# Where weights, bands and image buffers begin in memory: a convolution with an involution behind it, on one core

## The chip, the cores and the metric

The kernel runs on one core of a Trainium2 chip. Times are microseconds (us) on the device; the kernel before takes 1350.81 us, the median of three runs. The core has a matrix engine (TensorE, "PE" in the profile, its weight loads "PEld"), VectorE ("DVE"), ScalarE ("ACT"), GpSimd ("POOL") and SyncE ("SP"). 16 DMA engines move data between DRAM and the on-chip memory SBUF, which has 128 partitions.

## The reference

Two layers over 32 images of 256 channels and 32 x 32 pixels, in float32. The first normalizes groups of 8 channels, rounds to half precision, and adds a 3 x 3 convolution. The second makes from its own input, for every pixel and each of 16 groups of channels, the 49 weights of a 7 x 7 window, and sums the window with them (an involution):

```python
x = x + conv3x3(_gn(x))                                   # 256 -> 256 channels, quantized
v = _gn(x)
y = relu(bn(einsum('oc,bchw->bohw', w1, v)))              # 64 channels
w = einsum('oc,bchw->bohw', w2, y) + b2                   # 16 groups x 49 weights a pixel
patches = [pad(v, 3)[:, :, i:i+H, j:j+W] for i in range(7) for j in range(7)]
x = x + einsum('bgkhw,bgckhw->bgchw', w, patches)
```

## The kernel before

The first layer of one image, its second normalization and the transposing of its pixels (`front`) run a few steps ahead of the second layer. One loop over `n` (L559) deals out the work by hand: in every other step a piece of the convolution (L332, 9 matmuls), the sums of one window (L525, 64 matmuls), weights of four rows (L414, 16 matmuls into each of two tiles), and, where due, transposes (L399) or the 64-channel product (L380). An image has `M` = 8 windows, one for each of `K` = 4 strips of 8 rows and two `SIDES` of 16 columns.

A sum over a window is made as a matmul: the contraction runs over pixels that give (partitions), and its moving operand is a band, which holds for every giving pixel the weights with which it enters the pixels around it. The weights must therefore be sheared, and this is done through DRAM:

- `weights` (L406) makes the weights in PSUM with one row of pixels on the partitions; `evict` (L427) adds the bias and places them in `w_sb`, a ring of 32 rows in SBUF with 160 floats (`WB`, 640 bytes) a row.
- `scatter` (L468) sends them to `wd` in DRAM, seven DMAs for each strip, all from SyncE (L479), 896 in all. One DMA takes 32 partitions and 8 rows, so 256 runs of 640 bytes. In `wd` a pixel has `WPIX` = 7 x 160 + 8 = 1128 floats (4512 bytes): seven rows of weights and eight zeros behind them.
- `load_bands` (L481) brings a strip back into one of three bands, with 16 DMAs (L500), two from SyncE and 14 from GpSimd. Each takes 8 rows and both sides, 16 runs of up to 1128 floats. Row `r` begins `2 r` floats ahead of its pixel, which shifts the weights by that many places; what is then read before the pixel is the zeros behind its neighbour. Successive DMAs of GpSimd share eight semaphores: the ninth waits until the first has landed.

A band has, on each side, room for 22 columns of 160 floats; a window uses 19 of them (`WINI`): columns 3 to 21 on side 0 and 0 to 18 on side 1. `sums` (L511) picks them with `j0`. The ring and the bands are filled with zeros once by GpSimd (L144, L196, L198), and three DMAs write the zeros in `wd` that are never overwritten (L191). `x_tiles` holds five images of 8192 bytes a partition; `load_x` fills one with two DMAs (L106), `add_windows` (L541) adds the sums to it, and `store` (L546) writes it out in two halves.

SyncE's queue takes, in order of issue, scatters, two loads of each band, loads of x and stores. The addresses of the program before, in bytes within a partition: bands at 14048, 42272 and 70496, the ring at 117152, the x buffers from 172896 on in steps of 8192. `wd` begins at 81920 in DRAM.

Of the kernel before, what the change touches and what calls it, by code (L numbers as in the profile page):

```python
# [9 lines left out]
F32 = mybir.dt.float32  # L10
# [3 lines left out]
P = 128  # L14
B, C, H, W = 32, 256, 32, 32
# [5 lines left out]
K1, PAD1 = 7, 3  # L21
# [15 lines left out]
XR = 4  # L37
RG = 2
KP = P // RG
TR = RG * XR  # L40
SIDES = 2
JC = W // SIDES
K = H // TR
M = K * SIDES
WIN = XR + K1 - 1
WINC = JC + K1 - 1
WINI = JC + PAD1

V = 2
A = G // V
WB = G * WIN
PAD = V * (TR - XR)
WPIX = K1 * WB + PAD
SW = K1 * G
S = H + 2 * PAD1
T = 4
# [2 lines left out]
PAIRS = G // 2  # L62
ROW = S * WPIX
WR = 4
NBAND = 3
# [13 lines left out]
def tile_quant_conv_then_involution(  # L79
# [10 lines left out]
    nc = tc.nc  # L90
    PSUM = bass.MemoryType.PSUM

    const = ctx.enter_context(tc.tile_pool(name="const", bufs=1))
# [45 lines left out]
        nc.gpsimd.memset(t, 0.0)  # L139

    y_sb = [const.tile([P, N // 2], F32, name=f"y_{i}") for i in range(2)]
    bands = [const.tile([P, SIDES, WINC * WB + PAD], F32, name=f"band_{i}") for i in range(NBAND)]
    for t in bands[CH:]:
        nc.gpsimd.memset(t, 0.0)  # L144
    pixels = [const.tile([P, 2, PAIRS, PAIR], F32, name=f"pixels_{i}") for i in range(NPIX)]
# [4 lines left out]
    w_sb = const.tile([P, 2, RING, A, WIN, V], F32, name="w_sb")  # L150
    wd = dram.tile([H, S, WPIX], F32, name="wd")
    acc = [ps_acc.tile([P, RG, NT], F32, name=f"acc_{d}") for d in range(SIDES)]
# [15 lines left out]
    w2_sb = late_sb[:, : K1 * SW].rearrange("p (k n) -> p k n", n=SW)  # L168
    b2_sb = late_sb[:, K1 * SW :].rearrange("p (e r n) -> p e r n", r=2, n=SW)

    bn_ve = const.tile([P, 1], F32, name="bn_ve")
    nc.vector.tensor_scalar(bn_ve, bn[:, 3:4], BN_EPS, None, ALU.add)
    bn_r = rsqrt(bn_ve, [P, 1], "bn")
# [5 lines left out]


    for col, cols, at, n in (
        (0, S, K1 * WB, PAD),
        (PAD1, PAD1, 0, PAD1 * WB),
        (W, PAD1, (K1 - PAD1) * WB, PAD1 * WB),
    ):
        to = bass.AP(
            tensor=wd.tensor,
            offset=wd.offset + col * WPIX + at,
            ap=[[ROW, H], [WPIX, cols], [1, n]],
        )  # L190
        nc.sync.dma_start(to, bands[NBAND - 1][:H, 0, :n].unsqueeze(1).to_broadcast([H, cols, n]))  # L191
# [276 lines left out]
    def scatter(b, k, part):  # L468

        at = (b * H + k * TR) % RING  # L470
        for dj in range(part, K1, 2):
            t, e = divmod(dj, 2)
            to = bass.AP(
                tensor=wd.tensor,
                offset=wd.offset + k * TR * ROW + dj * WPIX + (K1 - 1 - dj) * WB,
                ap=[[WPIX, TW], [ROW, TR], [1, WB]],
            )
            rows = w_sb[t * TW : (t + 1) * TW, e, at : at + TR]
            nc.sync.dma_start(to, rows.rearrange("p s a r v -> p s (a r v)"))  # L479

    def load_bands(b, k):  # L481

        band = bands[(b * K + k) % NBAND]
        side = WINC * WB + PAD
        for i, j in enumerate(ORDER):
            cut = max(0, PAD1 - j)
            n = (K1 - cut) * WB + PAD
            src = bass.AP(
                tensor=wd.tensor,
                offset=wd.offset + k * TR * ROW + (j + PAD1) * WPIX + cut * WB,  # L490
                ap=[[ROW - V, TR], [(W - 1 - 2 * j) * WPIX - cut * WB, SIDES], [1, n]],
            )
            to = band[j::JC]
            to = bass.AP(
                tensor=to.tensor,
                offset=to.offset + (j + cut) * WB,
                ap=[to.ap[0], [side + (JC - 1 - 2 * j - cut) * WB, SIDES], [1, n]],
            )
            queue = nc.sync if j in BY_SYNC else nc.gpsimd
            queue.dma_start(to, src)  # L500

    def windows(b, m):


        k, d = divmod(m, SIDES)
        for g in range(RG):
            top = k * TR + g * XR - PAD1
            at = acc[d][:, g, : CH * WINI * WIN].rearrange("p (h j r) -> p h j r", h=CH, r=WIN)
            yield g, at, top, max(top, 0), min(top + WIN, H)

    def sums(b, m):  # L511

        k, d = divmod(m, SIDES)
        j0 = 0 if d else PAD1
        band = bands[(b * K + k) % NBAND][:, d]
        px = pixels[(b * K + k) % NPIX][:, d]
        for h in range(CH):
            for v in range(2):
                for g, at, top, f, l in windows(b, m):
                    p = slice(g * KP, (g + 1) * KP)  # L520
                    of = band[p, V * g * XR + j0 * WB : V * g * XR + (j0 + WINI) * WB]
                    of = of.rearrange("p (j a r v) -> p j a r v", a=A, r=WIN, v=V)
                    for t in range(T):
                        a = h * T + t
                        nc.tensor.matmul(  # L525
                            at[t * TW : (t + 1) * TW, h, :, f - top : l - top],
                            px[p, a, v * GC : v * GC + TW],
                            of[:, :, a, f - top : l - top, v],
                            start=(h, v) == (0, 0),
                            stop=(h, v) == (CH - 1, 1),  # L530
                        )

    def add_windows(b, m):
# [4 lines left out]
        for g, at, top, f, l in windows(b, m):  # L538
            x_at = to[:, :, f:l, j0 : j0 + WINI]
            of = at.rearrange("p h j r -> p h r j")[:, :, f - top : l - top]  # L540
# [11 lines left out]
    def due(n, lag):  # L552

        b, i = divmod(n - lag, per)
        return (b, i) if 0 <= b < B else (None, None)

    with tc.manual_schedule():
        fronts = {}
        for n in range(FRONT, B * per + 2):  # L559
            b, i = due(n, FRONT)  # L560
# [12 lines left out]
            b, i = due(n, 0)  # L573
            if b is not None and i % 2 == 0:
                sums(b, i // 2)
            b, i = due(n, 1)
# [6 lines left out]
            b, i = due(n, 2)  # L583
            if b is not None and i == 2 * (M - 1 - SIDES):
                store(b, 0)
            b, i = due(n, -LEAD)
# [3 lines left out]
            for part in range(2):  # L590
                b, i = due(n, -LEAD + 1 + part)
                if b is not None and i % 2 == 0:
                    for k in range(K):
                        if i // 2 == min((k + 1) * TR // WR, H // WR - 1):
                            scatter(b, k, part)
            b, i = due(n, LOAD)
# [3 lines left out]
            b, i = due(n, 3 - 4 * NBAND)  # L600
            if b is not None and i % 4 == 0:
                load_bands(b, i // 4)
# [38 lines left out]
```

## Time and profile before

| what | value |
|---|---|
| three runs | 1348.24, 1350.81, 1355.07 us |
| the profiled execution | 1362.92 us, span 1361.1 us |
| mean granted TensorE clock | 0.98 |
| GpSimd's issues of bands (L500) | 1792, 549 ns each, 980.4 us |
| from such an issue to landing | median 4.5 us (2.5 to 8.6) |
| scatter issues on SyncE (L479) | 896, 160 KB each, median 526 ns |
| HBM | 176.60 MB read, 180.76 MB written |

The profile is of one execution. A share of busy time is an average; which resource sets the time of a stretch is read from what ended the waits there. "Issue" in a list of waits means that nothing in the trace held the engine.

### The profile page before, as it was taken

To read this page: it belongs to the slowest core of one execution; us is meant where nothing else is said; L and a number is where in the kernel's file an instruction comes from. 1 tells how busy PE (TensorE), PEld (TensorE's weight loads), DVE (VectorE), ACT (ScalarE), POOL (GpSimd) and SP (SyncE) were. 2 spreads that over 40 slices of the span, in tenths; PEclk is the share of its full clock that TensorE was granted. 3 is DMA by queue.
4 is the path that set the end of the run, shared out by engine and by line. 5 is a ranking of instruction groups with operands and counts; after the bars stand their busy time and mean duration, and the time that the engine had idled before them with its cause. 6 is when DMAs were issued, how large, how long until landed. Compare 5 with 4: busy or idle time off the path is not lost.

```text
span 1361.1 us, 69383 instructions
## 1 busy us (share of the span) xinstructions
PE 1264.5 (93%) x29440; PEld 808.0 (59%) x29440; DVE 819.7 (60%) x2539; ACT 733.2 (54%) x1731; POOL 1014.4 (75%) x1818
## 2 busy tenths in 40 slices
PE   5899999999999999999999999999999999999765
PEld 2455666665656665665666566666666665666543
DVE  3465666565657665665566566666666665666542
ACT  6765656455655555655456555546555554653300
POOL 9067877777786786787778777777777777888785
PEclk9999999999999999999999999999999999999986
DMA  6099999999999999999999999999999999999995
GB/s 225 20 250 254 280 270 288 281 278 265 280 267 271 289 278 270 282 281 270 284 272 288 264 280 291 283 282 280 278 290 276 270 276 288 278 291 263 268 269 170
DMA packets 360738, 362.08 MB, mean 266 GB/s; under 512 B 75056, under 2 KB 304752, under 8 KB 359152
## 3 DMA queue, kind: packets, MB, share of 16 engines
q1 hardware_dynamic: 278512, 229.38, 56.2%
q0 software_dynamic: 81920, 128.28, 33.4%
q8 instruction: 234, 3.83, 1.2%
q14 instruction: 72, 0.59, 0.1%
HBM read 176.60 MB, written 180.76 MB: 263 GB/s over the span
## 4 chain that ended last, share of the span: by engine, by line
PE 72%; DMA 15%; issue 4%; POOL 3%; ACT 3%; DVE 2%; SPq 0%; POOLq 0%; DVEq 0%; ACTq 0%
PE pc L332 30%; PE acc L525 23%; PE pw L414 13%; DMA band<-wd 10%; PE py L380 4%; DMA wd<-w_sb 4%; PE pt L399 3%; POOL band L500 3%; ACT junk L214 1%; DVE w_sb L438 1%; DMA band<-in_w 1%; DVE x L541 0%; ACT xn L273 0%; DMA out<-x 0%; ACT xq L273 0%
## 5 line engine op out<-in xcount | busy, mean ns | idle before, releaser
L500 POOL DMA_DIRECT2D band<-wd x1792 | 980.4, 549 | 333.3 <-DMA band<-wd 186.8
L438 DVE TENSOR_TENSOR w_sb<-pw,late_sb 128x224 f32<-128x224 f32 (+7 forms) x1280 | 331.1, 323 | 425.3 <-PE pw L414 425.0
L332 PE MATMUL pc<-xq,wq 128*128 128x496 f16 (+3 forms) x2304 | 540.1, 381 | 23.1 <-ACT xq L273 18.5
L525 PE MATMUL acc<-band,pixels 64*32 64x190 f32 (+1 forms) x16384 | 426.2, 331 | 38.6 <-DMA band<-wd 18.2
L332 PEld LDWEIGHTS <-wq 128*128 128x128 f16 x2304 | 207.6, 99 | 320.5 <-issue 109.0
L525 PEld LDWEIGHTS acc<-band,pixels 64*32 64x32 f32 x16384 | 301.2, 107 | 128.5 <-issue 82.6
L414 PE MATMUL pw<-late_sb,y 64*32 64x224 f32 (+1 forms) x8192 | 286.2, 329 | 24.1 <-issue 23.7
L541 DVE TENSOR_TENSOR x<-acc,x 128x380 f32<-128x380 f32 (+1 forms) x512 | 262.5, 513 | 35.3 <-PE acc L525 26.4
L414 PEld LDWEIGHTS pw<-late_sb,y 64*32 64x32 f32 x8192 | 184.4, 105 | 51.8 <-issue 36.9
L403 ACT COPY pixels<-pt 128x512 f32<-128x512 f32 x128 | 73.7, 576 | 247.7 <-PE pt L399 247.7
L214 ACT ACTIVATE junk<-x 128x512 f16<-128x512 f32 (+1 forms) x192 | 146.4, 762 | 14.5 <-DVE x L348 12.0
L214 ACT ACTIVATE junk<-x,mean 128x1024 f16<-128x1024 f32 x128 | 147.1, 1149 | 4.3
L245 ACT ACTIVATE s<-back,eps 128x2 f32<-128x2 f32 x64 | 18.9, 296 | 183.9 <-DVE back L230 183.9
L346 DVE TENSOR_SCALAR q<-pc 128x512 f16<-128x512 f32 x128 | 87.3, 682 | 21.7 <-PE pc L332 21.6
L273 ACT ACTIVATE xn<-x,off,rstd 128x512 f32<-128x512 f32 x128 | 96.2, 800 | 0.0
L348 DVE SCALAR_TENSOR_TENSOR x<-q,early_sb,x 128x512 f32<-128x512 f16 x128 | 94.6, 739 | 0.3
L399 PEld LDWEIGHTS pt<-ident,xn 128*128 128x128 f32 x512 | 64.4, 143 | 29.4 <-issue 6.2
L399 PE MATMUL pt<-ident,xn 128*128 128x128 f32 x512 | 78.7, 277 | 2.5 <-issue 2.4
L273 ACT ACTIVATE xq<-x,off,rstd 128x1024 f16<-128x1024 f32 x64 | 75.7, 1227 | 1.0 <-PE pc L332 1.0
L380 PEld LDWEIGHTS py<-xn,early_sb 128*64 128x64 f32 x2048 | 62.7, 138 | 17.3 <-ACT mean L235 8.5
L380 PE MATMUL py<-xn,early_sb 128*64 128x64 f32 x2048 | 67.6, 224 | 3.3 <-ACT xn L273 2.2
L235 ACT ACTIVATE mean<-back 128x2 f32<-128x2 f32 x64 | 12.5, 196 | 101.4 <-DVE back L230 101.4
(40 smaller groups left out, 380.0 us busy)
## 6 DMA issues: line engine op xcount, KB each, us to landing
wd<-w_sb SPq DMA_DIRECT2D x896, 160.0 KB
band<-wd POOLq DMA_DIRECT2D x1664, 70.5 KB, 4.6
x<-in_x SPq DMA_DIRECT2D x64, 512.0 KB
out<-x SPq DMA_DIRECT2D x64, 512.0 KB
band<-wd POOLq DMA_DIRECT2D x128, 60.5 KB, 4.5
band<-wd SPq DMA_DIRECT2D x128, 50.5 KB
band<-wd SPq DMA_DIRECT2D x128, 40.5 KB
band<-in_w SPq DMA_DIRECT2D x2, 1152.0 KB
```

The lines of the kernel that those rows point to most:

```text
L214: nc.scalar.activation(junk[:, n0:n1], src[:, h, n0:n1], func, bias=bias, accum_out=self.sums[:, i : i + 1])
L273: nc.scalar.activation(dst, src, AF.Identity, bias=self.off[:, one], scale=self.rstd[:, one])
L332: nc.tensor.matmul(pc.rearrange("p (r c) -> p r c", c=W)[:, r0 - nt * RT : r1 - nt * RT, c0:c1], wq[:, kh, k, mh * P : (mh + 1) * P], xq[: ...
L346: nc.vector.tensor_scalar(q, pc, F16_MAX, -F16_MAX, ALU.min, ALU.max)
L348: nc.vector.scalar_tensor_tensor(xt[:, mh, cols], q, bias_sb[:, mh : mh + 1], xt[:, mh, cols], ALU.add, ALU.add)
L380: nc.tensor.matmul(py[i * CR : (i + 1) * CR, cols], w1_sb[:, kh, :], px[:, r : r + 2], start=kh == 0, stop=kh == CH - 1,)
L399: nc.tensor.transpose(pt[:, i, h * P : (h + 1) * P], xn[:, h, (m + i) * P : (m + i + 1) * P], ident)
L414: nc.tensor.matmul(pws[i][t * TW : (t + 1) * TW, : dj.stop - dj.start, r], y_sb[b % 2][half, (r0 // 2 + r) * W : (r0 // 2 + r + 1) * W], w ...
L438: nc.vector.tensor_tensor(to, of[:, :, d0:d1], bias[:, :, d0:d1], ALU.add)
L500: queue.dma_start(to, src)
L525: nc.tensor.matmul(at[t * TW : (t + 1) * TW, h, :, f - top : l - top], px[p, a, v * GC : v * GC + TW], of[:, :, a, f - top : l - top, v], ...
L541: nc.vector.tensor_tensor(x_at, of, x_at, ALU.add)
```

## The change

`WPIX` becomes 1152 floats (4608 bytes, 18 x 256), and all of `wd` is shifted by `FROM` = 16 floats (64 bytes). The zeros behind a pixel are now 32 floats; they are written for the columns from the one ahead of the image to its last. A band's side gets `SIDE` = 3072 floats and holds just the 19 columns that are used, so that `j0` goes away. Two small tiles that nothing reads, `gap` and `gap2`, move what is allocated after them: bands now begin at 14080, 38656 and 63232, the ring at 106240, and the x buffers at 162304 and in steps of 8192, all of them multiples of 256. The bytes that scatters, bands, loads and stores move stay the same.

```diff
@@ -43,8 +43,8 @@
 WIN = XR + K1 - 1
-WINC = JC + K1 - 1
 WINI = JC + PAD1
+SIDE = 3072
@@ -53,7 +53,8 @@
 PAD = V * (TR - XR)
-WPIX = K1 * WB + PAD
+WPIX = 1152
+FROM = 16
@@ -139,7 +140,9 @@
-    bands = [const.tile([P, SIDES, WINC * WB + PAD], F32, name=f"band_{i}") for i in range(NBAND)]
+    gap = const.tile([P, 8], F32, name="gap")
+    nc.gpsimd.memset(gap, 0.0)
+    bands = [const.tile([P, SIDES, SIDE], F32, name=f"band_{i}") for i in range(NBAND)]
@@ -168,6 +171,8 @@
+    gap = const.tile([P, 80], F32, name="gap2")
+    nc.gpsimd.memset(gap, 0.0)
@@ -179,13 +184,13 @@
     for col, cols, at, n in (
-        (0, S, K1 * WB, PAD),
+        (PAD1 - 1, W + 1, K1 * WB, WPIX - K1 * WB),
         (PAD1, PAD1, 0, PAD1 * WB),
         (W, PAD1, (K1 - PAD1) * WB, PAD1 * WB),
     ):
         to = bass.AP(
             tensor=wd.tensor,
-            offset=wd.offset + col * WPIX + at,
+            offset=wd.offset + FROM + col * WPIX + at,
@@ -472,7 +477,7 @@
-                offset=wd.offset + k * TR * ROW + dj * WPIX + (K1 - 1 - dj) * WB,
+                offset=wd.offset + FROM + k * TR * ROW + dj * WPIX + (K1 - 1 - dj) * WB,
                 ap=[[WPIX, TW], [ROW, TR], [1, WB]],
@@ -481,20 +486,19 @@
         band = bands[(b * K + k) % NBAND]
-        side = WINC * WB + PAD
         for i, j in enumerate(ORDER):
             cut = max(0, PAD1 - j)
             n = (K1 - cut) * WB + PAD
             src = bass.AP(
                 tensor=wd.tensor,
-                offset=wd.offset + k * TR * ROW + (j + PAD1) * WPIX + cut * WB,
+                offset=wd.offset + FROM + k * TR * ROW + (j + PAD1) * WPIX + cut * WB,
                 ap=[[ROW - V, TR], [(W - 1 - 2 * j) * WPIX - cut * WB, SIDES], [1, n]],
             )
             to = band[j::JC]
             to = bass.AP(
                 tensor=to.tensor,
-                offset=to.offset + (j + cut) * WB,
-                ap=[to.ap[0], [side + (JC - 1 - 2 * j - cut) * WB, SIDES], [1, n]],
+                offset=to.offset + (j + cut - PAD1) * WB,
+                ap=[to.ap[0], [SIDE + (JC - 1 - 2 * j - cut + PAD1) * WB, SIDES], [1, n]],
             )
@@ -511,14 +515,13 @@
         k, d = divmod(m, SIDES)
-        j0 = 0 if d else PAD1
@@
-                    of = band[p, V * g * XR + j0 * WB : V * g * XR + (j0 + WINI) * WB]
+                    of = band[p, V * g * XR : V * g * XR + WINI * WB]
```

## The prediction

> **What bounds the kernel now.** I read the page's busy table and slices first, then the DMA queues, the chain of waits, two tables of windows, TensorE's waits in the steady stretch, and the chain at the end. From the page (PE is TensorE's matmuls by slices of 34 us; q1 is what SyncE issues, q0 what GpSimd issues, q8 the fetching of instructions: packets, MB, share of 16 engines' span; last the chain of waits by engine):
>
> ```profile
> PE 1264.5 (93%) x29440; PEld 808.0 (59%) x29440; DVE 819.7 (60%) x2539; ACT 733.2 (54%) x1731; POOL 1014.4 (75%) x1818
> PE   5899999999999999999999999999999999999765
> DMA  6099999999999999999999999999999999999995
> q1 hardware_dynamic: 278512, 229.38, 56.2%
> q0 software_dynamic: 81920, 128.28, 33.4%
> q8 instruction: 234, 3.83, 1.2%
> PE 72%; DMA 15%; issue 4%; POOL 3%; ACT 3%; DVE 2%; SPq 0%; POOLq 0%; DVEq 0%; ACTq 0%
> ```
>
> Two resources are near full in nearly every slice, TensorE and the 16 DMA engines, and the chain gives 72% to TensorE. The windows part start, steady stretch and end (us from the start of the span, length, busy of PE, PEld, DVE, ACT and POOL, granted clock, DMA share, GB/s):
>
> ```profile
> 3.00:8.00 5.00, 0.00 (x0) 0.00 (x0) 0.61 (x3) 2.50 (x5) 5.00 (x2) 1.00 1.01 408
> 68.50:69.00 0.50, 0.50 (x4) 0.37 (x4) 0.40 (x3) 0.00 (x0) 0.00 (x0) 1.00 0.85 192
> 85.00:1250.00 1165.00, 1127.64 (x26611) 724.29 (x26611) 733.04 (x2284) 657.36 (x1557) 889.52 (x1627) 0.99 0.95 278
> 1250.00:1361.00 111.00, 74.43 (x2224) 53.27 (x2222) 49.55 (x145) 14.87 (x33) 80.40 (x147) 0.84 0.83 240
> ```
>
> From 85 to 1250 us TensorE is idle 1165 - 1127.64 = 37.4 us, the most that any faster transfer can give back there; DMA has 5% of 1165 = 58 us of slack. What ended TensorE's idle time there (total, times, longest):
>
> ```profile
> PE pw L414 <- issue: 17.6, 17, 2.4
> PE acc L525 <- issue: 7.8, 12, 1.9
> PE acc L525 <- DMA band<-wd: 4.6, 8, 1.0
> PE pc L332 <- issue: 3.0, 3, 2.0
> PE pt L399 <- issue: 2.4, 1, 2.4
> ```
>
> Only 4.6 us wait openly for a band. 17.6 + 7.8 + 3.0 + 2.4 = 30.8 us are "issue", in few pieces of up to 2.4 us: nothing in the program holds TensorE. I read them as late instructions, for q8 brings 234 packets on the same loaded engines. In the end stretch the chain is another (start us, us, what):
>
> ```profile
> 1288.80 3.55 DMA wd<-w_sb
> 1292.36 2.17 POOL band L500 x4
> 1294.53 3.61 DMA band<-wd
> ...
> 1299.14 3.65 DMA wd<-w_sb
> ...
> 1311.23 3.18 DMA band<-wd
> ...
> 1324.21 5.13 DMA wd<-w_sb
> ```
>
> There a scatter of weights, its way back as a band and the sums follow each other with no cover. From 1283 us to the end the chain's DMA shares are 18.5% bands, 15.8% scatters and 4.7% stores: 39% of 78 us, 30 us.
>
> [...] the first scatters read just these, and in the 68.50:69.00 window they ran at 192 GB/s, while loads over all partitions ran at 408 GB/s (3.00:8.00). [...] in the trace's packet records 180,014 of 229,376 packets of 640 B took exactly 32 ns whatever their start, and the undisturbed packets of all sizes lie on one line, about 8.6 ns and 27.2 B per ns (4096 B: 159 ns; 9216 B: 347 ns; 4928 B: 189 ns), although these begin at 96, 224, 32 and 192 past a multiple of 256. [...]
>
> **The change part by part.** Instructions, their order and their waits are the same on every engine but for two small memsets and smaller memsets of the bands. What changes is addresses.
>
> Scatters (L468 to L479): 896 DMAs of 32 x 8 = 256 runs of 640 B. The ring began at byte 117152, 160 past a multiple of 256, and its rows are 640 B, so reads began at 160 or 32 past one[...]. It now begins at 106240, a multiple of 256: 0 or 128[...]. [...] Their writes begin at multiples of 64 B rather than of 32 B (pixel pitch 4608 for 4512 B). No view prices that, and the packet records show no step.
>
> Bands (L481 to L500): 2048 DMAs, 16 runs of mostly 4512 B. Row r begins 8 r bytes before its pixel; before, a start could lie on any multiple of 8 in 256 B[...]; now it lies 8 to 64 past a multiple of 256[...]. [...] For j = 15 the two pixels no longer adjoin, so 128 DMAs read 16 runs rather than 8: 1,024 more packets at 9 ns (a 4 B packet) is 0.6 us per engine, and GpSimd's 549 ns an issue I leave as they are.
>
> x and out: buffers went from 96 past a multiple of 256 to 0. Loads ran at 408 GB/s before, so I give them nothing. [...]
>
> Sum: 17.9 + 7.4 + 3.8 - 0.6 = 28.5 us per engine, 2.3% of the 0.911 x 1361 = 1240 us that the queues' shares make. Bounds: nothing, if the flat packet times are the whole truth; above, all that packets take beyond the line: (35.6 - 32) ns x 229,376 and (240 - 174) ns x 24,576, over 16 engines 52 + 101 = 153 us, if it were all due to addresses. [...]
>
> The memsets: a band is 6144 words for 7056, 5.97 us become 5.2, three times; GpSimd's first band goes out at 71.9 us and SyncE's padding (L191), which waits for a memset, is followed only by loads not used for tens of us. Nothing on the path. The padding's runs become 1056 of 128 B for 1216 of 32 B, once. PE and VectorE read the same shapes with the same steps: I take nothing[...].
>
> On the path: 1165 of 1361 us of the saving, 24 us, fall in the steady stretch, where slack grows from 58 to 82 us. I let waits for transfers shrink as 1/slack: 30.8 + 4.6 = 35.4 us become 35.4 x 58 / 82 = 25.0, that is -10.4. In the end stretch 2.3% of 30 us is -0.7. What is late next is TensorE itself, which nothing here shortens. Sum -11.1 us on the profiled execution's 1362.9: 1351.8. That execution was 12.1 us above the runs' median of 1350.81; in proportion the forecast is 1351.8 x 1350.81 / 1362.92 = 1339.8, say 1340.
>
> **The rivals.** (a) [...] engines already take 32 ns a packet and TensorE is 97% busy. For it: the flat packet times. [...] Time 1350 less the end's few tenths, 1349.
> (b) [...] half of the 153 us goes, 76 us per engine, so slack more than doubles; 35.4 us of waits become 35.4 x 58 / (58 + 65) = 16.7, and 6% of the end's 30 us go as well: -18.7 - 1.8 = -20.5, or 1330; with the rest of the end's idle time (111 - 74.4 us, a fifth of it) 1323. For it: a band packet's mean is 240 ns for a median of 174. Against: loads from x show the same excess beside the scatters (207 for 159 ns), which speaks for two queues sharing an engine.
> (c) Slower. Every pixel now begins on the same place modulo 256, with a pitch of 18 x 256 B, where 4512 B spread the starts over all of it; if memory takes such a regular stride worse, write packets grow. [...] The point: 58 us of slack, or 68 over the span, is 68 x 16 / 229,376 = 4.7 ns on a packet of 35.6. At 16% (5.7 ns, 82 us, 70 of them steady) the engines need 1107 + 70 = 1177 of 1165 us, and the end some 2 more: +14, or 1365.
>
> **How the numbers follow.** The forecast 0.38, own range 1333 to 1344; (a) 0.27; (b) 0.15; (c) 0.20. By 0.5% (6.8 us), which is about what a measurement tells from no change: faster 0.38 + 0.15 = 0.53, same 0.27, slower 0.20. The range 1322 to 1363 takes in (a), (b) and the near part of (c), and leaves out about 0.12 above and 0.06 below.
>
> **What would show it.** Right: DMA share in 85 to 1250 us near 0.93, mean times of the 640 B and 4512 B packets down by some per cent, TensorE's "issue" near 22 us for 30.8, matmul times unchanged. (a): these stay. (b): band packets' mean falls towards 174 ns. (c): q1's share above 56.2% at the same bytes, and TensorE waiting openly for bands. I am wrong in my reading of "issue" if the DMA share falls and these pieces stay.

## The result, and the profile after

The change makes the kernel slower: the median is 1363.96 us (1363.07 to 1368.74) for 1350.81 before (1346.91 to 1355.07), five runs each; the ratio is 1.0092, 95% interval 1.0066 to 1.0119. The forecast was 1340. 1363.96 lies just outside its range.

The page of the profiled execution after (1368.74 us, span 1367.0), the parts that answer to those shown of before:

```profile
PE 1262.7 (92%) x29440; PEld 807.0 (59%) x29440; DVE 825.0 (60%) x2539; ACT 734.2 (54%) x1731; POOL 1009.0 (74%) x1820
PE   5899999999999999999999999999999999999755
DMA  6099999999999999999899999999999899998995
q1 hardware_dynamic: 278352, 229.47, 55.8%
q0 software_dynamic: 83968, 128.29, 33.2%
q8 instruction: 234, 3.83, 1.2%
PE 63%; DMA 21%; issue 5%; POOL 4%; ACT 3%; DVE 2%; SPq 2%; POOLq 0%; ACTq 0%
```

TensorE is busy for the same time as before (1262.7 for 1264.5 us), so no matmul got slower. The DMA queues' shares are nearly what they were, 55.8% and 33.2% for 56.2% and 33.4%, of a longer span. Packets didn't get longer either: in the packet records the mean is 35.3 ns for 35.6 with 640 bytes, 237 for 240 with 4512. In the chain TensorE's part falls from 72% to 63% and that of transfers rises from 15% to 21%, but this says little of the loss: among the kernels below, the slower SBUF half has 81% and 7%, and `bands_256`, which loses nothing, 64% and 19%. The steady stretch in windows and TensorE's waits in it, in the order of before:

```profile
85.00:1250.00 1165.00, 1123.71 (x26456) 719.84 (x26453) 731.39 (x2282) 658.16 (x1558) 886.00 (x1622) 1.00 0.95 277
```

```profile
PE acc L528 <- issue: 14.1, 16, 3.0
PE pw L419 <- issue: 14.0, 18, 2.3
PE acc L528 <- DMA band<-wd: 6.1, 6, 2.1
PE pc L337 <- issue: 3.4, 4, 1.2
PE acc L528 <- DVE q L351: 1.9, 2, 1.6
...
PE pt L404 <- issue: 0.3, 1, 0.3
```

The DMA share stays at 0.95, TensorE is idle for 41.3 us rather than 37.4, and "issue" stays too (14.1 + 14.0 + 3.4 + 0.3 = 31.8 us for 30.8). These differences of 1 to 4 us are smaller than those between executions of one kernel (1346.91 to 1355.07 us before). So one pair of profiles shows what did not happen, much shorter packets and fewer waits, but can't place 13 us. Which part costs is for the experiments to show.

One view does show an effect of the addresses at once. Early in the kernel the first scatters run while hardly any other data moves. A window of 0.8 us from the first packet on, before and then after (the last number is GB/s):

```profile
64.97:65.77 0.80, 0.80 (x26) 0.60 (x30) 0.75 (x2) 0.56 (x2) 0.00 (x0) 1.00 0.81 181
```

```profile
66.61:67.41 0.80, 0.80 (x27) 0.60 (x30) 0.75 (x2) 0.56 (x2) 0.00 (x0) 1.00 0.85 203
```

With hardly any other transfer beside them, the first scatters, which read partitions 0 to 63, run 12% faster after the change. The kernel is slower nonetheless.

### The profile page after: what moved, and what is told of

Same layout as the page of the kernel before. It is cut to its first block, busy times and chain, and to the rows that moved or that the text cites. A ratio compares the mean times of both kernels' runs of the same rounds, so it can differ in the third digit from the quotient of the medians.

```text
span 1367.0 us, 69385 instructions
## 1 busy us (share of the span) xinstructions
PE 1262.7 (92%) x29440; PEld 807.0 (59%) x29440; DVE 825.0 (60%) x2539; ACT 734.2 (54%) x1731; POOL 1009.0 (74%) x1820
## 3 DMA queue, kind: packets, MB, share of 16 engines
q1 hardware_dynamic: 278352, 229.47, 55.8%
q0 software_dynamic: 83968, 128.29, 33.2%
## 4 chain that ended last, share of the span: by engine, by line
PE 63%; DMA 21%; issue 5%; POOL 4%; ACT 3%; DVE 2%; SPq 2%; POOLq 0%; ACTq 0%
PE pc L337 26%; PE acc L528 20%; DMA band<-wd 14%; PE pw L419 12%; DMA wd<-w_sb 5%; POOL band L504 4%; PE py L385 3%; PE pt L404 3%; SPq L484 1%; ACT junk L219 1%; DVE w_sb L443 1%; DMA out<-x 1%; DMA x<-in_x 1%; ACT xn L278 1%; DMA band<-in_w 0%
## 5 line engine op out<-in xcount | busy, mean ns | idle before, releaser
L419 PE MATMUL pw<-late_sb,y 64*32 64x224 f32 (+1 forms) x8192 | 289.1, 331 | 19.2 <-issue 17.1
L544 DVE TENSOR_TENSOR x<-acc,x 128x380 f32<-128x380 f32 (+1 forms) x512 | 262.0, 512 | 31.8 <-PE acc L528 22.9
```

The source lines that it names most:

```text
L419: nc.tensor.matmul(pws[i][t * TW : (t + 1) * TW, : dj.stop - dj.start, r], y_sb[b % 2][half, (r0 // 2 + r) * W : (r0 // 2 + r + 1) * W], w ...
L544: nc.vector.tensor_tensor(x_at, of, x_at, ALU.add)
```

## The experiments

Every kernel below was run beside the kernel before on the same chip, in 6 to 22 executions; ratios are to before, with their 95% intervals. "Places" are the byte at which a buffer begins in a partition, modulo 256.

**First: DRAM or SBUF.** The change falls into two halves. One run has only the DRAM edits:

```diff
-WPIX = K1 * WB + PAD
+WPIX = 1152
+FROM = 16
...
-        (0, S, K1 * WB, PAD),
+        (PAD1 - 1, W + 1, K1 * WB, WPIX - K1 * WB),
...
+  FROM added to the offsets of L188, L475 and L490
```

> Pitch of 1152 floats and the shift by 16 in DRAM alone; bands, ring and x buffers where they were before. Theory A (the pitch of 18 x 256 bytes in DRAM makes scatters and bands later): ratio to before near 1.009, as for the whole change. Theory B (the places in SBUF do it): 1.000 within 0.3%. Theory C (neither; every small change of addresses or of the start moves the random stalls): anywhere within 1%, with no order among the parts.

The other, called the SBUF half below, has only the rest, `SIDE` and the two gaps:

> Bands of 3072 floats a side and the two gaps, so bands, ring and x buffers begin at multiples of 256; DRAM with its pitch of 1128 floats. Theory A: 1.000 within 0.3%. Theory B: near 1.009. Theory C: anywhere within 1%.

A third takes another pitch in DRAM in the kernel before, `WPIX = 1136` with `FROM = 0`:

> Before with a pixel pitch in DRAM of 1136 floats, 71 x 64 bytes, and no shift: all scatters begin at multiples of 64 bytes, but the pixels' starts still spread over the four places modulo 256. Theory A: about 1.000, since the stride is not regular modulo 256; if it is slower as well, it is the 64 bytes or the longer pitch and not the regular stride. Theory B: 1.000. Theory C: anywhere within 1%.

Measured: the DRAM half 1.0025 (1.0003 to 1.0048), the SBUF half 1.0088 (1.0060 to 1.0115), the pitch of 1136 floats 0.9994 (0.9973 to 1.0015). The SBUF half had six executions; the plain ratio of its median, 1353.35, to that of all executions of before on that chip, 1346.04, is 1.0054, so 1.0088 may be high. Theory A is refuted as the main cause, though the pitch of 18 x 256 bytes with its shift may carry a quarter of a per cent. That scatters begin at multiples of 64 bytes in DRAM gained nothing here (0.9994).

**Second: which part of SBUF.** The bands' shape, multiples of 64 and the x buffers were taken apart. The first run is before plus the first gap:

```diff
+    gap = const.tile([P, 8], F32, name="gap")
+    nc.gpsimd.memset(gap, 0.0)
     bands = [const.tile([P, SIDES, WINC * WB + PAD], F32, name=f"band_{i}") for i in range(NBAND)]
```

> Before with only the first gap of 32 bytes ahead of the bands: everything behind it moves by 32 bytes, bands of 3528 floats a side with the three unread columns; the bands begin at 0, 64 and 128 past a multiple of 256, the ring at 192, x at 128, all multiples of 64. Theory B1 (multiples of 64 in SBUF are what costs): near 1.009. Theory B2 (the bands' shape, 3072 floats a side without the unread columns, costs, wherever they begin): 1.000. Theory B3 (x buffers at multiples of 256 cost): 1.000.

The next two keep the new bands, drop both gaps and leave DRAM as before, the second with `SIDE = 3048`:

> Bands of 3072 floats a side without unread columns, but neither gap: bands, ring and pixels at 224 past a multiple of 256 and x at 160, all 32 past a multiple of 64; DRAM as before. B1: 1.000. B2: near 1.009. B3: 1.000.

> As the run without gaps, but a side of 3048 floats, just what is used: sides 12192 bytes apart, not a multiple of 64, bands at 224, 32 and 96 past a multiple of 256 and ring and x at 160 and 96, as before. B1: 1.000. B2 through the three columns that are gone: near 1.009; B2 through the distance of 12288 bytes between sides: 1.000. B3: 1.000.

The last drops `gap2` alone from the SBUF half:

> The change's places in SBUF without the second gap: bands, pixels and ring at multiples of 256, x at 192 past one; DRAM as before. B1 and B2: near 1.009. B3: 1.000.

Measured: 1.0003 (0.9979 to 1.0026), 0.9993 (0.9967 to 1.0019), 0.9990 (0.9970 to 1.0010), and 1.0067 (1.0044 to 1.0091). The unread columns and the bands' shape are free, B2 falls. The x buffers aren't needed for the loss, B3 falls. B1 in its form of multiples of 64 falls as well, for the ring at 192 and the bands at 0, 64 and 128 cost nothing. Common to the slow kernels are multiples of 256.

**Third: bands, ring or x at multiples of 256.**

```diff
+    gap2 = const.tile([P, 40], F32, name="gap2")
+    nc.gpsimd.memset(gap2, 0.0)
     pixels = [const.tile([P, 2, PAIRS, PAIR], F32, name=f"pixels_{i}") for i in range(NPIX)]
```

behind the changed bands, in place of the later `gap2`, gives the first; a gap of 24 floats at the same spot in the kernel before the second; a first gap of 24 floats rather than 8, with no second, the third; a gap of 40 floats ahead of L171 in the kernel before the fourth. DRAM is as before in all four.

> Bands as in the change (3072 floats a side, beginning at multiples of 256, so every band packet lands at a multiple of 64), and a gap behind them that puts pixels and ring back to 160 and x to 96 past a multiple of 256; DRAM as before. Theory D1 (bands at multiples of 64 or 256 on both sides cost): near 1.008. D2 (ring, pixels and conv weights at multiples of 256 cost): 1.000. D3 (it takes several of them together): in between.

> Before with a gap of 96 bytes between bands and pixels: pixels, ring and conv weights begin at multiples of 256, x at 192 past one; bands with their shape and places of before. D1: 1.000. D2: near 1.008. D3: in between.

> The change's SBUF without the second gap, but with a longer first gap: bands, pixels, ring and conv weights begin 64 past a multiple of 256, x at a multiple of 256. If the multiples of 64 cost (band packets on both sides at multiples of 64): near 1.008. If it takes multiples of 256 (or of 128): 1.000.

> Before with a gap of 160 bytes ahead of the x buffers only: these begin at multiples of 256, all else stays. D1 and D2: 1.000. If the places of x carry a part of their own: 1.002 to 1.004.

Measured: bands 1.0007 (0.9985 to 1.0028); pixels, ring and convolution weights 1.0058 (1.0035 to 1.0081); all of it at 64 rather than at 0 0.9982 (0.9962 to 1.0001); x 0.9986 (0.9965 to 1.0007). D2 holds, and theory C doesn't: the loss comes with one place and not at random.

**Fourth: the ring, from both sides.** In the kernel before, only the ring moves:

```diff
+    gap = const.tile([P, 24], F32, name="gap")
+    nc.gpsimd.memset(gap, 0.0)
     w_sb = const.tile([P, 2, RING, A, WIN, V], F32, name="w_sb")
+    gap2 = const.tile([P, 40], F32, name="gap2")
+    nc.gpsimd.memset(gap2, 0.0)
```

> Before with a gap of 96 bytes ahead of the ring and one of 160 bytes behind it: only the ring moves, from 160 past a multiple of 256 to a multiple of 256; pixels, convolution weights and x keep their places modulo 256. Theory E1 (the ring's start, so the scatters' reads, is the cause): near 1.006, first 256 scatter packets in 0.80 us rather than 0.91. E2 (pixels or convolution weights): 1.000.

And in the changed kernel only the ring moves away, with gaps of 16 and 48 floats around it:

> The whole change with the ring alone moved to 64 past a multiple of 256. E1: what is left is the DRAM part, 1.000 to 1.004. E2: 1.009 as with the whole change.

Measured: 1.0057 (1.0028 to 1.0085) and 1.0045 (1.0025 to 1.0064), where the whole change has 1.0092. E1 holds: 96 bytes ahead of one buffer make the larger part of the loss, and taking the ring off its place gives about half of the loss back. The second is a little more than the expectation's 1.000 to 1.004, with an interval that reaches into it. What stays there fits the DRAM half (1.0025, whose interval overlaps), and 1.0057 x 1.0025 = 1.0082 lies within the interval of the whole. Whether the pitch or the shift makes that rest was not tried. VectorE, which writes the ring, isn't what the place costs: in the profiles its median is 377 ns a write before and 376 ns with the ring alone moved.

The same early window in the run with the ring alone, and in the one with all at 64:

```profile
64.70:65.50 0.80, 0.80 (x26) 0.60 (x30) 0.76 (x2) 0.55 (x2) 0.00 (x0) 1.00 0.85 202
```

```profile
64.49:65.29 0.80, 0.80 (x27) 0.60 (x30) 0.75 (x2) 0.56 (x2) 0.00 (x0) 1.00 0.84 181
```

The quick scatter goes with the ring, and so does the loss. Over the whole run the scatters are quicker too, though by less: SyncE gets them issued sooner, and their packets are shorter. SyncE's scatter issues (shortest, median and longest, ns; first and last start, us) in the kernel before and with the ring alone at a multiple of 256:

```profile
L479 SPq DMA_DIRECT2D wd<-w_sb x896: 302/526/2683, 64.1 to 1331.6; - x180
```

```profile
L483 SPq DMA_DIRECT2D wd<-w_sb x896: 302/499/2584, 63.9 to 1323.5; - x180
```

The median is 488 to 513 ns in all six kernels with two steps a strip and the ring at a multiple of 256, and 518 to 541 in the twelve others, the kernel before among them. In the packet records, with the pitch of before, the 640-byte packets' mean is 34.9 to 35.2 ns with the ring there (six kernels) and 35.5 to 35.9 with it elsewhere (nine).

What these scatters delay is harder to see. The pages' lists of issues (KB each, median us from issue to landing) have for the bands, in the kernel before, with the ring alone at a multiple of 256, and with all at 64:

```profile
band<-wd POOLq DMA_DIRECT2D x1664, 70.5 KB, 4.6
```

```profile
band<-wd POOLq DMA_DIRECT2D x1664, 70.5 KB, 4.8
```

```profile
band<-wd POOLq DMA_DIRECT2D x1664, 70.5 KB, 4.6
```

The five kernels with the old order of scatters that have the ring at a multiple of 256 have 4.7 or 4.8, and those without it 4.6 where the page has a value. But the traces tell the landing of only 224 to 672 of GpSimd's 1792 band reads, and GpSimd's wait for landed bands does not follow the loss. Before, the ring alone, the SBUF half (slower) and all at 64 (not slower):

```profile
POOL band L500 <- DMA band<-wd: 186.8, 238, 3.6
```

```profile
POOL band L504 <- DMA band<-wd: 197.8, 248, 3.0
```

```profile
POOL band L503 <- DMA band<-wd: 186.5, 254, 2.9
```

```profile
POOL band L501 <- DMA band<-wd: 196.9, 242, 3.5
```

So that bands land later is a hint, and not shown to be the way by which the time is lost.

**Fifth: is it the bursts?** Quicker scatters could take the engines from the bands in bursts. Two runs deal a strip's scatters out over four steps. The same edit makes successive ones read other halves of the partitions:

```diff
-        for dj in range(part, K1, 2):
+        for dj in range(part, K1, 4):
...
-            for part in range(2):
+            for part in range(4):
                 b, i = due(n, -LEAD + 1 + part)
```

> Before with each strip's seven scatters dealt out over four steps (2, 2, 2, 1) instead of two (4, 3). If bursts of scatters hold up bands: somewhat faster than before, 0.995 to 1.000; the last scatters come two steps later, which may cost as much.

> The same spreading with the ring at a multiple of 256. Theory F1 (quicker scatters cost as bursts): the 0.6% between ring places shrinks to under 0.3% against the spread run with the ring where it was. F2 (the transfers get worse however they are spread): the difference stays near 0.6%.

Measured: 1.0485 (1.0450 to 1.0521) and 1.0492 (1.0452 to 1.0531). The first expectation is far off, 65 us of loss. A strip's last scatters come two steps later. TensorE's waits of the steady stretch with the ring at its old place:

```profile
PE acc L525 <- DMA band<-wd: 33.5, 12, 5.0
PE acc L525 <- issue: 17.1, 16, 2.0
PE pw L414 <- issue: 13.7, 13, 2.2
```

33.5 us rather than 4.6 now wait openly for bands, 29 of the 65 us; the rest isn't placed. Between the two the ring makes 0.1%, as F1 has it, but each interval is 0.4% wide to a side and another wait rules, so this pair doesn't decide.

**Sixth: quick scatters without moving the ring.** Successive scatters read other halves of the partitions (0 to 63 and 64 to 127 by turns), with the same two steps a strip:

```diff
-        for dj in range(part, K1, 2):
+        for dj in ((0, 4, 2, 6), (1, 5, 3))[part]:
```

> Before with the scatters of a strip in the order 0, 4, 2, 6 and 1, 5, 3 instead of 0, 2, 4, 6 and 1, 3, 5, so that successive ones read other halves of the partitions; the ring stays at 160. The first 768 scatter packets of the run should be through sooner than in 2.49 us. Theory F1 (quicker scatters are what costs, however they became quicker): 1.003 to 1.006. F3 (the cost belongs to reads that begin at 0 and 128, not to speed): 1.000 or faster.

> The same order with the ring alone at a multiple of 256. F1: no better than the ring alone, 1.006 to 1.010. F3: 1.006 as the ring alone, or what the order gains taken from it; against alt_before 0.6% slower.

Measured: 1.0012 (0.9982 to 1.0042) and 1.0122 (1.0073 to 1.0172). By the packet records the first 768 packets begin within 2.16 us for 2.49 before, quicker even than with the ring alone (2.25), and no loss can be measured. With the ring moved as well the kernel is about 1.1% slower than that. But the order makes only the start quicker. Over the whole run its scatter issues take as long as before,

```profile
L479 SPq DMA_DIRECT2D wd<-w_sb x896: 302/524/2407, 63.6 to 1321.7; - x180
```

and its 640-byte packets 35.5 ns in the mean for 35.6, where the ring alone has 499 and 35.1. So beyond the start, where nearly all of the time is spent, the order made the scatters no quicker that could be seen, and this run says little of F1. The cost does not come with quick first scatters alone; whether it comes with quicker scatters throughout (F1) or with reads at 0 and 128 as such (F3) stays open.

**Last: the harmless parts together.**

> The parts that cost nothing, together: a pixel pitch of 1136 floats without the shift, bands of 3072 floats a side, and bands, pixels, ring and convolution weights 64 past a multiple of 256 with x at a multiple of 256. If small gains of the single runs (0.9994 and 0.9982) are real and add: 0.997 to 0.998. If they are noise: 1.000.

Measured: 0.9993 (0.9972 to 1.0014). The single values below 1 don't add up to a gain; no version tried beats the kernel before.

## Why the prediction was wrong

- *What bounds the kernel.* TensorE near full and DMA at 0.95 was right, and the matmuls stayed as they were. That transfers matter at the margin was right too; a strip's scatters two steps later cost 4.8%.
- *From cheaper packets to slack and fewer waits.* This step failed, in size and then in sign. The prediction took 17.9 us per engine off the scatters, 7.4 off the bands and 3.8 off the stores for their new starts; these were the author's assumptions, and no trace showed that a start has such a price. It let slack grow with the sum from 58 to 82 us, and waits of 35.4 us shrink to 25.0. With the whole change the packets' mean fell by 0.3 of 35.6 ns, 0.3 x 229,376 / 16 = 4.3 us per engine; the DMA share stayed at 0.95, and "issue" was 31.8 us for 30.8. With the ring alone the packets fell by 0.5 ns, some 7 us per engine, and the kernel still became 0.57% slower. So less packet time did not become less waiting. That the ring's new starts could cost anything the prediction put at nothing, and they made the larger part of the loss. The savings were also priced at the rate of loads that ran alone (408 GB/s), and used where two queues share the engines (56.2% and 33.4% of their time).
- *The new starts by themselves.* The undisturbed scatters did become quicker, 203 GB/s for 181, so for these the sign was right. But starts at 64 and 192 gave the same 181 as 32 and 160. The 192 GB/s of the prediction were read in half a microsecond of a later scatter; from the first packet on it was 181.
- *Waits as 1/slack.* Slack did not grow, so whether "issue" would follow the DMA share was not tested, nor whether it is late instructions.
- *Bands and stores.* 7.4 and 3.8 us per engine were expected. The band packets' mean is 237 for 240 ns, the bands alone at multiples of 256 make 1.0007, x alone 0.9986: no gain that can be measured. GpSimd's queue has 2,048 packets more, 83,968 for 81,920, where 1,024 were expected.
- *Memsets, unread columns, padding at nothing:* right, 0.9990 and 0.9993 without the gaps.
- *Rival (a),* no gain where it matters, names what most parts did: seven of the runs with one part or a variant of it lie within 0.2% of 1. *Rival (c)* had the right side and, by luck, nearly the right time, 1365, but the wrong place: the regular pitch in DRAM was to add 14 us through longer write packets; the DRAM half adds 0.25%, 3.4 us, and its 640-byte packets have 35.9 ns for 35.6, not 5.7 ns more. The larger part comes from a buffer for which no rival had a loss, since its reads were counted as cheaper, and by themselves were (202 GB/s for 181).

What stays open is how reads that begin at 0 and 128 modulo 256 lengthen the kernel. The runs show that it is these starts: 0 and 128 gave 1.0057 with nothing else moved, while 64 and 192 gave 0.9982 and 1.0003, and 96 and 224 gave 0.9993, beside the 32 and 160 of before. Nothing in the traces tells what the transfers meet on their way, and later landing is no sure sign: with the alternating order the bands' median is 4.7 us and the time still 1.0012.

## What to carry to other kernels

A change that makes a transfer quicker by itself can still make the kernel slower, as here (202 GB/s for 181 in the first scatters, 1.0057 in the whole, at a DMA share of 0.95); price it in the stretch where it runs, or leave both bounds in, a loss included. When a change moves many addresses, undo it buffer by buffer: here the loss came with 96 bytes ahead of one tile, and most other parts did nothing. For a per cent, one pair of profiles isn't enough; look in them for what did not change, and let repeated runs say which part costs.

## What the runs showed of the hardware that wasn't expected

- The commonest time of a packet was the same before and after: 32 ns for 640 bytes (180,014 and 182,897 of 229,376 packets, with starts at 32 and 160, then 0 and 128), 159 ns for 4096 bytes (4,563 and 5,157 of 8,192 packets, into x at 96, then 0).
- The rate of the first scatters, which read the same half of the partitions one after the other, was not: 181 GB/s with starts at 32 and 160 or 64 and 192, 202 to 203 with 0 and 128.
- These quicker starts cost 0.6% of a kernel whose DMA share is 0.95, and with the alternating order about 1.1%, give or take 0.3 and 0.6%.
- Multiples of 64 bytes, in DRAM or in SBUF, rather than of 32, gave nothing that could be measured (0.9994, 0.9982, 1.0003).
